# Seven products of a block's first matrix joined in PSUM accumulators instead of on VectorE, in a cross-attention block

## The chip, the core and the metric

The kernel runs on one core of one Trainium2 chip. The time is the device time of the program in microseconds (us); less is better. The runs before the change have a median of 803.14 us (801.75 to 804.53). A core has TensorE (PE, matrix products into the PSUM buffers), VectorE (DVE), ScalarE (ACT), GpSimd (POOL) and SyncE (SP), which here issues most of the DMAs. Each engine works through its own queue in order; semaphores tie them together.

## The reference

A cross-attention block for 4 batches of 512 rows, width 512, 16 heads of 32, inner width 2048, all in float32:

```
x = layer_norm(hidden, ln1_w, ln1_b)
q, k, v = x @ q_w + q_b, enc @ k_w + k_b, enc @ v_w + v_b      # 16 heads of 32
attn = softmax(where(mask, q k^T / sqrt(32), min))
hidden = (attn v) @ cproj_w + cproj_b + hidden
y = layer_norm(hidden, ln2_w, ln2_b)
y = gelu(y @ fc_w + fc_b, approximate=True)                    # 512 -> 2048
out = hidden + y @ proj_w + proj_b                             # 2048 -> 512
```

The change touches `gelu(y @ fc_w + fc_b)`.

## The kernel before

**Attention.** The work is cut into 16 windows, w = 4 * batch + head group (four heads each), and each window into four units of 128 rows, qt; unit u = 4 w + qt runs from 0 to 63. A unit (`scores`, L255, and `turn`, L274) does four score products on TensorE into one PSUM tile of four banks, which has one buffer (pool ps_sc). For each head VectorE adds the mask and takes the row minimum in one reduction (L266), and ScalarE takes the exponential (L270). VectorE transposes two heads at a time (L285, L293); after an odd unit it takes reciprocals (L290), which ScalarE spreads (L292, "rr"). DMAs on SP (L328) exchange blocks of 32 rows, and `attend` (L331, TensorE "av") multiplies by v some units later.

**Filler.** TensorE's other work is put between the units by hand: lists `first[w]` and `later[w]` hold steps with a cost. Where `first[w]` is a tuple it has one list for each unit, run after that unit's scores and turn. Steps are the k, q and v projections (L213 to L234), cproj (L382), the transposes of the second layer norm (L420), and pieces of the feed-forward part: `mlp`, a list of fc and proj steps of batch 0 and of half of batch 1 (SPLIT = 1, FIRST = 2), taken by `some(n)` (a pair counts as two). In windows 13 to 15 these are the only filler. One step of fc makes a tile of 128 of the 2048 columns (`fc`, L532: four products, 512 rows wide, then Gelu on ScalarE); one step of proj makes 128 rows.

**A pair by seven products.** Batch 0's fc, and all fc after attention, take two column tiles at once (`fc_seven`, L483) by Strassen's scheme in Winograd's form: the 512 x 256 block of weights and the 512 x 512 block of y are cut in 2 x 2, and seven half-size products take the place of eight. The sums of weights s1 to s4 are made by `a_sums` (on GpSimd in attention, called by `fc_sums`, L520; on VectorE after it, `sum_wa`, L580), the sums of y, t1 to t4, by `y_sums` (L472), once for a batch. The seven results go to four PSUM tiles, ScalarE copies the first to SBUF (L498), and VectorE joins them by four adds into g (L455); ScalarE's Gelu follows in place (L513). A product is four matmuls in the profile, a pair 28, all with L495 (in `product`).

PSUM: `ps_acc` has four banks for all filler and av; after attention four more, `ps_last`, take the place of the scores.

**Order of weights.** `load_mlp` (L437) loads the tiles of fc and proj in the order of use into a ring of eight, each when the product that last read its place is done; `fc_sums` keeps the weight sums up to two pairs ahead, as soon as the raw weights are asked for.

**After attention** (`last_mlps`, L590): the other half of batch 1's fc and all of batches 2 and 3, pair by pair, each batch followed by its projection, also by seven products (`project`, L613). `load_wa` loads raw weights two pairs ahead.

Of the kernel before, what the change touches and what calls it, by code (L numbers as in the profile page):

```python
# [52 lines left out]
def xattn_block(ctx: ExitStack, tc: tile.TileContext, x, encT, mask, q_w, k_w, v_w, c_w, fc_w, p_w, vecs, rows, out):  # L53
# [201 lines left out]
    def scores(w, qt):  # L255
# [7 lines left out]
        for h in range(HG):  # L263
# [7 lines left out]
            if h % 2:  # L271
                S["ps", w, qt, h // 2] = score_pair()

# [123 lines left out]
    def load_hid(b, ts_):  # L397

        for t in ts_:
            if ("hid", b, t) not in S:  # L400
                S["hid", b, t] = hids.tile([P, D], F32, tag="hid", name=f"hid_{b}_{t}")
            Q[0].dma_start(out=S["hid", b, t], in_=S["xa", b][ts(t, P), :])
        for t in ts_:
# [68 lines left out]
    def y_sums(b):  # L472
        y11, y12, y21, y22 = y_blocks(b)
        e = nc.vector if b else nc.gpsimd
        sub(ys[:, 0], y12, y11)
        sub(ys[:, 1], y22, ys[:, 0])
        sub(y12, y22, y12, e)
        sub(ys[:, 2], y21, ys[:, 1], e)
# [4 lines left out]
    def fc_seven(b, c, g, a, s, half):  # L483
# [4 lines left out]
        q1, q26 = (acc_half(f"{n}_{b}_{c}") for n in ("q1", "q26"))  # L488
        q57, q34 = (half(f"{n}_{b}_{c}") for n in ("q57", "q34"))
        p1 = small.tile([P, HL], F32, tag="p1", bufs=1, name=f"p1_{b}_{c}")  # L490
        g = g.rearrange("p i (j l) -> p (i j) l", j=2)

        def product(o, x, y):
            for k in range(2):
                nc.tensor.matmul(o, x[:, k], y[:, k], start=(k == 0), stop=(k == 1))  # L495

        product(q1[:, 0], a[0][:, 0:2], y11)
        nc.scalar.copy(p1, q1[:, 0])  # L498
        product(q26[:, 0], a[0][:, 2:4], y21)
        product(q26[:, 1], s2, t2)  # L500
        add(nc.vector, g[:, 0:4:3], q26, p1[:, None, :].broadcast_to([P, 2, HL]))
        product(q57[:, 1], s3, t3)
        product(q57[:, 0], s1, t1)
        u2 = g[:, 3:4]
        add(nc.vector, g[:, 1:3], q57, u2.broadcast_to([P, 2, HL]))
        add(nc.vector, g[:, 3], q57[:, 0], g[:, 2])
        product(q34[:, 0], s4, y22)
        product(q34[:, 1], a[1][:, 2:4], t4)
        add(nc.vector, g[:, 1:3], q34, g[:, 1:3])
        for i in range(2):  # L510
            f = 2 * c + i
            h = g[:, 2 * i : 2 * i + 2]
            nc.scalar.activation(h, h, AF.Gelu_apprx_tanh, bias=vec[:, FCB + f : FCB + f + 1], scale=1.0)  # L513

    fc_pairs = [(b, c) for b in range(SPLIT) for c in range(NP)]
# [461 lines left out]
```

## Time and profile before

The profile is of one execution, which took 801.93 us.

| | |
|---|---|
| median of the runs | 803.14 us |
| the profiled execution | 801.93 us, its span 800.2 us |
| mean granted TensorE clock | 0.998 |
| VectorE, line L455 joining a pair in attention (8 pairs) | 3 adds of 512 columns (0.658, 0.692, 0.692 us), 1 of 256 (0.424) |
| VectorE, the same after attention (20 pairs) | 0.684, 0.692, 0.692 and 0.425 us |
| ScalarE, copy of 256 columns out of PSUM (L498) | 0.355 us each, 28 |
| ScalarE, copy of 512 columns out of PSUM (L245) | 0.577 us each, 16 |
| ScalarE, Gelu of 512 columns (L513, L537) | 0.714 and 0.686 us |
| ScalarE, table loads | 1.283 us each, 30 |
| GpSimd, one sum of weights (256 columns) | 0.735 to 0.750 us |
| TensorE, matmul to matmul, 512 and 256 columns | 0.429 and 0.215 us |

In the profile a line is a group of instructions: line, engine, operation, what it writes and reads, shape, count, then busy time and the mean of one in ns, and the idle time just before them with what ended it. Mean durations overlap by some tenths of a microsecond within an engine (matmuls, and the steps of VectorE and ScalarE, are pipelined), so that start to start counts where instructions follow one another. A timeline line begins with start and length in us.

### The profile page before, as it was taken

What the parts mean: (1) busy time and instruction counts of PE and PEld (TensorE: products, weight loads), DVE (VectorE), ACT (ScalarE), POOL (GpSimd) and SP (SyncE); (2) the same over time, 40 slices, a digit from 0 to 9 for tenths busy, and PEclk for the clock granted to TensorE, in tenths of its full rate; (3) what the DMA queues carried; (4) which work ended last, traced back from release to release, by engine and by line L of the source; (5) the groups of instructions that cost most, each with busy time, mean ns of one, the idle gap of its engine ahead of it and who ended that gap; (6) DMA issues with size and microseconds to landing.
All of it is one profiled execution on the core that took longest, in us unless ns stands there. A gap on an engine that the chain in (4) does not pass through costs nothing.

```text
span 800.2 us, 12085 instructions
## 1 busy us (share of the span) xinstructions
PE 785.3 (98%) x4178; PEld 499.4 (62%) x4178; DVE 573.8 (72%) x1179; ACT 339.5 (42%) x745; POOL 123.9 (15%) x146
## 2 busy tenths in 40 slices
PE   9999999989999999999999999999999999999998
PEld 6545455456655645556553433446888888888887
DVE  3789998888888857779878988546738983368511
ACT  2567765547763636456554479500201220022100
POOL 1210030055121141001220100020040020200011
PEclk9999999999999999999999999999999999999999
DMA  8889999847897777787777799882325330033001
GB/s 325 289 230 241 235 237 244 231 115 182 209 240 196 211 210 192 179 198 199 181 173 213 205 261 246 202 254 93 117 84 172 118 106 14 27 86 86 1 14 40
DMA packets 60957, 137.15 MB, mean 171 GB/s; under 512 B 12464, under 2 KB 15664, under 8 KB 60768
## 3 DMA queue, kind: packets, MB, share of 16 engines
q1 hardware_dynamic: 59472, 132.43, 61.3%
q0 software_dynamic: 896, 2.82, 1.1%
q10 hardware_dynamic: 528, 1.14, 0.7%
q8 instruction: 33, 0.54, 0.3%
q14 instruction: 28, 0.23, 0.1%
HBM read 58.22 MB, written 6.82 MB: 81 GB/s over the span
## 4 chain that ended last, share of the span: by engine, by line
PE 87%; DVE 6%; SPq 3%; ACT 1%; issue 1%; DMA 1%; POOL 0%; DVEq 0%; POOLq 0%; ACTq 0%
PE q L495 20%; PE accp L554 8%; PE sc L262 7%; PE accc L386 7%; PE av L345 7%; PE accv L240 6%; PE acck L218 6%; PE accq L228 5%; PE accf L536 3%; DVE ptt L266 3%; SPq L328 2%; PE q4p L622 2%; PE q3p L622 2%; PE q5p L622 2%; PE q6p L622 2%; PE q7p L622 2%
## 5 line engine op out<-in xcount | busy, mean ns | idle before, releaser
L270 ACT ACTIVATE ptt<-ptt,mn 128x512 f32<-128x512 f32 x256 | 181.7, 711 | 135.1 <-DVE mn L266 134.8
L266 DVE CUSTOM_DVE_ANT_0 ptt<-sc,mb 128x512 f32<-128x512 f32 x256 | 161.0, 685 | 32.7 <-PE sc L262 32.4
L285 DVE STREAM_TRANSPOSE tb<-ptt 128x1024 f32<-128x1024 f32 x96 | 119.2, 1242 | 14.4 <-ACT ptt L270 12.9
L554 PE MATMUL accp<-pbt,gt 128*128 128x512 f32 x192 | 86.7, 600 | 0.0
L495 PE MATMUL q<-yT,gt 128*128 128x256 f32 x320 | 78.9, 379 | 0.0
L262 PE MATMUL sc<-pbt 32*128 32x512 f32 x512 | 73.0, 640 | 4.7 <-DVE mn L266 2.5
L513 ACT ACTIVATE ga<-ga,vec 128x512 f32<-128x512 f32 x40 | 26.7, 714 | 93.2 <-DVE ga L455 93.2
L495 PEld LDWEIGHTS q<-yT,gt 128*128 128x128 f32 x320 | 60.8, 190 | 8.7 <-issue 0.5
L554 PEld LDWEIGHTS accp<-pbt,gt 128*128 128x128 f32 x192 | 35.2, 190 | 49.0 <-issue 46.4
L240 PEld LDWEIGHTS accv<-ptt,xe 128*128 128x128 f32 x512 | 58.7, 192 | 9.5 <-issue 6.7
L495 PE MATMUL q<-ys,gt 128*128 128x256 f32 x240 | 61.8, 380 | 0.5 <-DVE ys L452 0.5
L240 PE MATMUL accv<-ptt,xe 128*128 128x128 f32 x512 | 60.8, 277 | 0.0
L218 PE MATMUL acck<-xe,ptt 128*128 128x512 f32 x128 | 59.1, 605 | 0.0
L228 PE MATMUL accq<-xe,ptt 128*128 128x512 f32 x128 | 58.4, 599 | 0.0
L386 PE MATMUL accc<-wc,oT 128*128 128x512 f32 x128 | 56.6, 596 | 0.0
L495 PEld LDWEIGHTS q<-ys,gt 128*128 128x128 f32 x240 | 45.4, 190 | 7.4 <-DVE ys L452 0.9
L345 PE MATMUL av<-pT,v 128*32 128x256 f32 x768 | 48.1, 392 | 1.8 <-DMA gt<-tb 0.7
L498 ACT COPY p<-q 128x256 f32<-128x256 f32 x28 | 9.9, 355 | 92.5 <-PE q L495 92.5
L270 ACT ACTIVATION_READ_ACCUMULATOR ptt<-ptt,mn 128x1 f32 x256 | 47.8, 187 | 0.0
L252 POOL TENSOR_TENSOR v<-v,row 128x512 f32<-128x512 f32 x16 | 20.4, 1275 | 172.9 <-ACT v L245 172.8
L228 PEld LDWEIGHTS accq<-xe,ptt 128*128 128x128 f32 x128 | 23.6, 190 | 32.4 <-issue 30.4
L262 PEld LDWEIGHTS sc<-pbt 32*128 32x128 f32 x512 | 20.0, 182 | 37.9 <-issue 21.4
(137 smaller groups left out, 1071.4 us busy)
## 6 DMA issues: line engine op xcount, KB each, us to landing
pT<-tb SPq DMA_DIRECT2D x384, 136.0 KB, 2.4
pbt<-p_w_dram SPq DMA_DIRECT2D x40, 256.0 KB, 3.1
gt<-fc_w_dram SPq DMA_DIRECT2D x40, 256.0 KB, 2.6
gt<-tb SPq DMA_DIRECT2D x64, 136.0 KB, 3.4
xe<-tb SPq DMA_DIRECT2D x56, 136.0 KB, 3.1
pbt<-fc_w_dram SPq DMA_DIRECT2D x24, 256.0 KB, 3.9
ptt<-k_w_dram SPq DMA_DIRECT2D x16, 256.0 KB, 3.8
xe<-encT_dram SPq DMA_DIRECT2D x16, 256.0 KB, 4.6
```

What stands on the lines that cost most here:

```text
L218: nc.tensor.matmul(acc, S["wk", w][:, d, :], eT[:, d, :], start=(d == 0), stop=(d == ND - 1))
L228: nc.tensor.matmul(acc, S["wq", w][:, d, :], xT[:, d, :], start=(d == 0), stop=(d == ND - 1))
L240: nc.tensor.matmul(acc[:, ts(t, P)], eT[:, d, ts(t, P)], S["wv", w][:, d, :], start=(d == 0), stop=(d == ND - 1),)
L262: nc.tensor.matmul(sc[:, h, :], qT[r, ts(qt, P)], kT[r, :], start=True, stop=True)
L266: nc.vector.tensor_tensor_reduce(out=s, in0=sc[:, h, :], in1=S["mb", w // NG], scale=1.0, scalar=FMAX, op0=ALU.add, op1=ALU.min, accum_out=mn,
L270: nc.scalar.activation(s, s, AF.Exp, bias=mn, scale=-1.0, accum_out=sums[:, qt, h : h + 1])
L285: nc.vector.transpose(*two_heads[k])
L345: nc.tensor.matmul(av[ts(h, HD), : 2 * P].rearrange(shape, **kw), v[:, t, ts(h, HD)], p[t][h], start=(t == 0), stop=(t == NT - 1),)
L386: nc.tensor.matmul(acc, S["oT", b][:, g, ts(t, P)], wc[:, g, :], start=(g == 0), stop=(g == NG - 1))
L495: nc.tensor.matmul(o, x[:, k], y[:, k], start=(k == 0), stop=(k == 1))
L554: nc.tensor.matmul(acc, gT[q % 2][:, k, ts(t, P)], S["pw", b, q * FQ + k], start=(k == 0), stop=(k == FQ - 1))
L622: nc.tensor.matmul(o[:, t], a[:, c, ts(t, P)], w[:, c], start=(c == pairs[0]), stop=(c == pairs[-1]))
```

## The change

Seven parts:

1. `fc_seven` joins the products in three PSUM tiles. qb takes s1 t1 and s3 t3; ScalarE copies both to g[2:4] (512 columns); then s4 y22 and (raw) t4 are added onto qb by TensorE. qa takes a11 y11; ScalarE copies that to g[0]; then a12 y21 is added onto qa. qc takes s2 t2. VectorE makes two adds (256 and 512 columns), GpSimd two (256 columns each). Gelu is three instructions (256, 256 and 512 columns), one of them straight out of PSUM.
2. It is a generator with one stop. `fc_start` runs it up to the stop: four products, the copy of qb, one add. `fc` runs the rest.
3. `scores` takes `middle`: after the second exponential the first step of the unit's list is started, if it is a pair.
4. Half of batch 1's fc (eight tiles in units 57 to 63) goes by pairs too, so that four steps take the place of eight. In windows 14 and 15 the lists become: unit 56 one step, 57 a pair, 58 a pair, 59 none, 60 a pair, 61 none, 62 a pair, 63 two steps. In unit 60 the pair stands behind a load in its list, so it isn't started early.
5. Batch 1's `y_sums` moves from after attention (VectorE) to unit 52 (GpSimd).
6. `fc_sums` issues weight sums when their pair is at most two products ahead of what is done, instead of when the weights are asked for.
7. The adds of proj's bias to rows of batch 1 on GpSimd (`hid_rows`) come one unit after their loads.

```diff
-    def scores(w, qt):
+    def scores(w, qt, middle=None):
...
             if h % 2:
                 S["ps", w, qt, h // 2] = score_pair()
+            if h == 1 and middle:
+                middle()
...
     def y_sums(b):
         y11, y12, y21, y22 = y_blocks(b)
-        e = nc.vector if b else nc.gpsimd
-        sub(ys[:, 0], y12, y11)
-        sub(ys[:, 1], y22, ys[:, 0])
-        sub(y12, y22, y12, e)
-        sub(ys[:, 2], y21, ys[:, 1], e)
+        e, o = ((nc.vector, nc.gpsimd), (nc.gpsimd,) * 2)[b] if b <= SPLIT else (nc.vector,) * 2
+        sub(ys[:, 0], y12, y11, e)
+        sub(ys[:, 1], y22, ys[:, 0], e)
+        sub(y12, y22, y12, o)
+        sub(ys[:, 2], y21, ys[:, 1], o)
...
-        q1, q26 = (acc_half(f"{n}_{b}_{c}") for n in ("q1", "q26"))
-        q57, q34 = (half(f"{n}_{b}_{c}") for n in ("q57", "q34"))
-        p1 = small.tile([P, HL], F32, tag="p1", bufs=1, name=f"p1_{b}_{c}")
+        qb, qa, qc = half(f"qb_{b}_{c}"), acc_half(f"qa_{b}_{c}"), acc_half(f"qc_{b}_{c}")
         g = g.rearrange("p i (j l) -> p (i j) l", j=2)
-
-        def product(o, x, y):
+        u2 = g[:, 0]
+
+        def product(o, x, y, clear=False):
             for k in range(2):
-                nc.tensor.matmul(o, x[:, k], y[:, k], start=(k == 0), stop=(k == 1))
-
-        product(q1[:, 0], a[0][:, 0:2], y11)
-        nc.scalar.copy(p1, q1[:, 0])
-        product(q26[:, 0], a[0][:, 2:4], y21)
-        product(q26[:, 1], s2, t2)
-        add(nc.vector, g[:, 0:4:3], q26, p1[:, None, :].broadcast_to([P, 2, HL]))
-        product(q57[:, 1], s3, t3)
-        product(q57[:, 0], s1, t1)
-        u2 = g[:, 3:4]
-        add(nc.vector, g[:, 1:3], q57, u2.broadcast_to([P, 2, HL]))
-        add(nc.vector, g[:, 3], q57[:, 0], g[:, 2])
-        product(q34[:, 0], s4, y22)
-        product(q34[:, 1], a[1][:, 2:4], t4)
-        add(nc.vector, g[:, 1:3], q34, g[:, 1:3])
-        for i in range(2):
+                nc.tensor.matmul(o, x[:, k], y[:, k], start=clear and k == 0, stop=k == 1, skip_group_check=not clear)
+
+        product(qb[:, 0], s1, t1, True)
+        product(qb[:, 1], s3, t3)
+        nc.scalar.copy(g[:, 2:], qb)
+        product(qa[:, 0], a[0][:, 0:2], y11, True)
+        product(qc[:, 0], s2, t2, True)
+        add(nc.gpsimd, g[:, 3], g[:, 2], g[:, 3])
+        yield
+        nc.scalar.copy(u2, qa[:, 0])
+        add(nc.vector, u2, qc[:, 0], u2)
+        add(nc.gpsimd, g[:, 3], g[:, 3], u2)
+        product(qb[:, 0], s4, y22)
+        product(qb[:, 1], a[1][:, 2:4], t4)
+        add(nc.vector, g[:, 1:3], qb, u2[:, None, :].broadcast_to([P, 2, HL]))
+        product(qa[:, 0], a[0][:, 2:4], y21)
+        for i, o, x in ((0, g[:, 1], g[:, 1]), (0, g[:, 0], qa[:, 0]), (1, g[:, 2:], g[:, 2:])):
             f = 2 * c + i
-            h = g[:, 2 * i : 2 * i + 2]
-            nc.scalar.activation(h, h, AF.Gelu_apprx_tanh, bias=vec[:, FCB + f : FCB + f + 1], scale=1.0)
-
-    fc_pairs = [(b, c) for b in range(SPLIT) for c in range(NP)]
+            nc.scalar.activation(o, x, AF.Gelu_apprx_tanh, bias=vec[:, FCB + f : FCB + f + 1], scale=1.0)
+
+    fc_pairs = [(b, c) for b in range(SPLIT + 1) for c in range(NP if b < SPLIT else FIRST * FQ // 2)]
...
-            if ("fcw", b, 2 * c + 1) not in S:
+            if products.index(("fc", b, *divmod(2 * c, FQ))) > count[1] + 2:
                 return
...
-    def fc(b, f):
...
-    def fc_by_pair(b, c):
+    started = {}
+
+    def fc_start(b, c):
+        if (b, c) in started:
+            return
         q, k = divmod(2 * c, FQ)
-        fc_seven(b, c, gT[q % 2][:, k : k + 2, :], raw_pair(b, c), S["ws", b, c], acc_half)
+        started[b, c] = fc_seven(b, c, gT[q % 2][:, k : k + 2, :], raw_pair(b, c), S["ws", b, c], acc_half)
+        next(started[b, c])
+
+    def fc(b, c):
+        fc_start(b, c)
+        list(started[b, c])
         count[1] += 2
...
-        y_sums(SPLIT)
-
         half = FIRST * FQ // 2
...
     def FC(b, q):
-        if b < SPLIT:
-            return [(2 * CHAIN * 7 / 8, lambda c=c: fc_by_pair(b, c)) for c in range(q * FQ // 2, (q + 1) * FQ // 2)]
-        return [(CHAIN, lambda f=f: fc(b, f)) for f in range(q * FQ, (q + 1) * FQ)]
+        return [(2 * CHAIN * 7 / 8, lambda c=c: fc(b, c), lambda c=c: fc_start(b, c)) for c in range(q * FQ // 2, (q + 1) * FQ // 2)]
...
-    first[13] = some(1), some(1) + stat(2, 0, 1), some(1) + stat(2, 2, 3) + rs(2), some(2)
-    first[14] = some(1) + norm(2, 0, 1), some(1) + norm(2, 2, 3), some(2), some(1)
-    first[15] = hid_(1, 2, 3) + some(1), some(1), some(1), some(2)
+    first[13] = do(lambda: y_sums(1)) + some(1), some(1) + stat(2, 0, 1), some(1) + stat(2, 2, 3) + rs(2), some(2)
+    first[14] = some(1) + norm(2, 0, 1), some(2) + norm(2, 2, 3), some(2), []
+    first[15] = hid_(1, 2, 3) + some(2), do(lambda: hid_rows(1, (2, 3))), some(2), some(2)
...
-            scores(w, qt)
+            now = work[qt] if by_unit else work
+            scores(w, qt, now[0][2] if now and len(now[0]) == 3 and (by_unit or qt < 2) else None)
```

More of the change, by code (lines that the diff above doesn't have):

```diff
@@ L395, in load_xn, with load_hid @@
             Q[0].dma_start(out=S["h", b, t], in_=S["xa", b][ts(t, P), :])
-    def load_hid(b, ts_):
+    def load_hid(b, ts_, rows=True):
         for t in ts_:
@@ L402, in load_hid, with hid_rows @@
             Q[0].dma_start(out=S["hid", b, t], in_=S["xa", b][ts(t, P), :])
+        if rows:
+            hid_rows(b, ts_)
+    def hid_rows(b, ts_):
         for t in ts_:
@@ L530, in fc_sums @@
             count[3] += 1
-    def fc(b, f):
-        q, k = divmod(f, FQ)
-        acc = acc_tile(f"accf_{b}_{f}")
-        for d in range(ND):
-            nc.tensor.matmul(acc, S["fcw", b, f][:, d, :], S["yT", b][:, d, :], start=(d == 0), stop=(d == ND - 1))
-        nc.scalar.activation(
-            gT[q % 2][:, k, :], acc, AF.Gelu_apprx_tanh, bias=vec[:, FCB + f : FCB + f + 1], scale=1.0
-        )
-        count[1] += 1
-        load_mlp()
-    def fc_by_pair(b, c):
-        q, k = divmod(2 * c, FQ)
-        fc_seven(b, c, gT[q % 2][:, k : k + 2, :], raw_pair(b, c), S["ws", b, c], acc_half)
+    started = {}
+    def fc_start(b, c):
+        if (b, c) in started:
+            return
+        q, k = divmod(2 * c, FQ)
+        started[b, c] = fc_seven(b, c, gT[q % 2][:, k : k + 2, :], raw_pair(b, c), S["ws", b, c], acc_half)
[3 more added lines that the diff above has]
+        list(started[b, c])
         count[1] += 2
@@ L609, in fc_pair @@
             sums()
-            fc_seven(b, c, ga[:, c], [wa[c % 2][:, i] for i in range(2)],
-                     [ws[c % 2][:, i] for i in range(4)], half_tile)
+            list(fc_seven(b, c, ga[:, c], [wa[c % 2][:, i] for i in range(2)],
+                     [ws[c % 2][:, i] for i in range(4)], half_tile))
         def project(b, pairs, sums, turns, middle):
@@ L756, in run @@
         while work and (budget is None or spent + work[0][0] / 2 <= budget):
-            cost, fn = work.pop(0)
+            cost, fn, *_ = work.pop(0)
             fn()
@@ L825, in hid_ @@
     def hid_(b, *ts_):
-        return do(lambda: load_hid(b, ts_))
+        return do(lambda: load_hid(b, ts_, False))
     def h_(b, *ts_):
@@ L888, in xattn_block @@
         by_unit = isinstance(work, tuple)
-        share = 0 if by_unit else sum(c for c, _ in work + rest) / NT
+        share = 0 if by_unit else sum(c[0] for c in work + rest) / NT
         due = 0.0
```

## The prediction

> **What bounds the kernel now.** First the page: shares of the engines, then the slices.
>
> ```profile
> span 800.2 us, 12085 instructions
> ...
> PE 785.3 (98%) x4178; PEld 499.4 (62%) x4178; DVE 573.8 (72%) x1179; ACT 339.5 (42%) x745; POOL 123.9 (15%) x146
> ...
> PE   9999999989999999999999999999999999999998
> ...
> DVE  3789998888888857779878988546738983368511
> ...
> PEclk9999999999999999999999999999999999999999
> ```
>
> TensorE is full in nearly every slice; VectorE is near full only in some, ScalarE and GpSimd nowhere. So a saving on VectorE is worth nothing by itself, and a wait put in front of TensorE costs its whole length, because TensorE has no slack later in which to catch up. Second, the chain in order of time gives the prices of TensorE's pieces (start, length).
>
> ```profile
> 173.35 3.61 PE av L345 x32
> ...
> 203.42 6.24 PE q L495 x28
> ...
> 468.29 7.06 PE accf L536 x16
> ...
> 478.29 3.63 PE accf L536 x8
> ```
>
> A pair by seven products is 6.24 us (28 matmuls, one each 0.215); two tiles in full are 7.06 to 7.26. Third, the timeline of the place where batch 1's first tiles run, unit 57 (start, length).
>
> ```profile
> 461.48 1.14 PE L262 MATMUL sc<-pbt 32*128 32x512 f32 x8
> ...
> 462.55 3.70 PE L536 MATMUL accf<-yT,pbt 128*128 128x512 f32 x8
> ...
> 464.57 0.68 DVE L266 CUSTOM_DVE_ANT_0 ptt<-sc,mb 128x512 f32<-128x512 f32 x1
> ...
> 465.30 0.72 ACT L270 ACTIVATE ptt<-ptt,mn 128x512 f32<-128x512 f32 x1 [3.74 <-DVE mn L266]
> ...
> 467.01 0.08 DVE L266 DVE_READ_ACCUMULATOR2_ANT mn<- 128x1 f32 x1
> ...
> 467.15 1.14 PE L262 MATMUL sc<-pbt 32*128 32x512 f32 x8 [0.90 <-DVE mn L266]
> ...
> 468.26 0.20 DVE L290 RECIPROCAL rsum<-sums 128x8 f32<-128x8 f32 x1
> 468.38 1.19 DVE L293 STREAM_TRANSPOSE tb<-ptt 128x1024 f32<-128x1024 f32 x1
> 468.50 0.40 ACT L292 COPY rr<-rsum 128x256 f32<-128x256 f32 x1 [0.27 <-DVE rsum L290]
> ```
>
> Three things are to be seen. The scores tile has one buffer: the next unit's scores (467.15) start only when the fourth reduction's accumulator is read (467.09), 2.5 us after the first reduction starts. What TensorE does meanwhile is the 3.6 us of other work placed between. And VectorE is already late here: scores end at 462.55, reductions start at 464.57. Exponentials start 0.73 after the first reduction and run 0.71 apart.
>
> **The change in units 57 to 63** (batch 1's fc). Removed: eight tiles, in the chain 6 x 3.63 + 7.06 = 28.8 us. Added: four pairs, 4 x 6.24 = 25.0. TensorE's work falls by **3.9**, and the 0.90 stall above goes, since 6.24 stands between those two scores. But eight pieces become four. They go to units 57, 58, 60 and 62, so units 59 and 61 have none: their scores are followed at once by the next scores, which must wait for four reductions. And each pair now has two waits of TensorE on ScalarE inside it: its fifth product accumulates onto the buffer that ScalarE's 512-wide copy reads (0.58, as L245's copy of that size), its seventh onto the one that the 256-wide copy reads (0.36, L498). The first copy stands in ScalarE's queue behind two exponentials (four in unit 60, where the work list begins with a load and so the early start doesn't apply); the second stands behind the other exponentials, and in odd units behind the rr copy, which waits for VectorE's reciprocal. By the row of 203.42 TensorE wants the fifth product 3.56 after the scores' end and the seventh 1.73 later. Going through it with these rows, in the times of the trace:
>
> - Unit 57: exponentials from 465.30, second ends 466.72, copy to 467.4; TensorE wants 466.1: waits 1.3. Exponentials end 468.8, reciprocal, rr copy 469.5, second copy 469.9 against 469.1: 0.8. Pair ends 470.85.
> - Unit 58: scores end 471.9. VectorE's transposes, two adds and two norms (0.98) put the reductions at 472.4; ScalarE has a table load, Gelus until 472.9, a table load (1.28) until 474.2, two exponentials, copy until 476.2; wanted at 475.45: 1.05 with the second copy. Pair ends 479, av (1.87), scores of 59 end 482.0.
> - Unit 60's scores wait for reductions 482.1 to 484.6: 2.7.
> - Unit 60: VectorE's transposes of unit 59 (2.8) hold its reductions to 487.5, the four exponentials end 491.1, copy 491.7, wanted 489.3: 2.4. Pair ends 494.3, scores of 61 497.2.
> - Unit 62's scores wait for reductions until 499.9: 2.6.
> - Unit 62: reductions 502.6 after transposes, copy 505.35, wanted 504.45: 1.1 with the second copy.
>
> Stalls: 2.1 + 1.05 + 2.7 + 2.4 + 2.6 + 1.1 = 12.0. Net **12.0 - 0.9 - 3.9 = +7.2**. After this TensorE runs projections without a wait, as before.
>
> **Batch 0's eight pairs** (units 22 to 45). The count of matmuls is the same. VectorE loses two 512-wide and one 256-wide add and gains one 256-wide (four adds, 2.5 us, become 1.1), ScalarE gains a 512-wide copy and splits a Gelu in two (512-wide: 0.71). A 256-wide Gelu out of PSUM has no row: 0.36 (copy of that size) to 0.71; 0.4 taken, the size decides. GpSimd gains two 256-wide adds (0.73 each): with batch 1's and the tail's 32 pairs, 47 us on an engine busy 124 of 800. They delay only the last Gelu; without that cover a Gelu would hold the next unit's exponentials by 0.7. Accumulating into a used bank is bounded by today's second matmuls of a product, which accumulate at the same 0.215: nothing. VectorE's relief hits no stall of TensorE, so it is worth nothing here. The same two copy waits apply: unit 23, straight after another pair, 0.65 + 0.9, so that av begins at 192.85 instead of 192.28, where its present wait of 0.69 for a buffer goes: 0.55; the odd units 25, 33, 37, 45 wait 0.2, 0.3, 0.35, 0.45 for the second copy behind rr. Sum **+1.9** (0 if ScalarE is earlier, 4 if every pair loses 0.5).
>
> **GpSimd's moved steps.** y_sums(1) goes from VectorE to GpSimd in unit 52, four ops of 1.26 to 1.78, 5.8 us, 30 us ahead of its reader; behind it stand the stores of out, whose adds come later anyway. Weight sums issued later (3.0 each): those of pair 0 stand behind the second store (issued 457.7) and end by 461.3, before 462.6. Pairs 2 and 3 sum at 474 and 480, needed at 485.8 and 500.9. The weights' loads keep their place in SP's queue (that of pair 0 issued at 453.02, landed 456.7). Row adds of hid come later, needed after 510. All nothing; a late one would cost its lateness.
>
> **Tail.** There ScalarE and VectorE have gaps, so the copies hide (copy done 2.4 into a pair, wanted at 3.5).
>
> ```profile
> PE tp L159 <- ACT pbt L231: 3.0, 1, 3.0
> PE sc L262 <- DVE mn L266: 2.5, 2, 1.6
> ...
> PE q L495 <- DVE ys L452: 0.5, 1, 0.5
> ```
>
> The last line's 0.5 goes (batch 1's sums are ready). The first projection matmul waits 0.4 at 575.8 for the last Gelu; the last add now lies before the last product, so that goes. But the first product is now s1 t1 instead of raw weights: at 601.2, batch 2's start, VectorE ends the first weight sum at 602.33, so TensorE loses 1.15. Batch 3's start has 2 us to spare. Sum **+0.25**.
>
> **Sum**: 7.2 + 1.9 + 0.25 = +9.3. On the profiled execution (801.93, span 800.2, 1.7 around it) that is 811.3; it stands 1.2 under the median of the runs, 803.14, so the forecast is **811**.
>
> **Half clock.** The waits above show one TensorE gap of 3.0; the windows show what followed (the number before the last two is the granted clock).
>
> ```profile
> 80.00:100.00 20.00, 18.35 (x124) 9.57 (x120) 18.64 (x44) 14.32 (x37) 1.27 (x1) 1.00 0.93 235
> 160.00:180.00 20.00, 16.94 (x114) 10.58 (x113) 16.51 (x36) 8.82 (x19) 11.57 (x13) 0.91 0.45 114
> ```
>
> After the gap of 3.0 the clock fell (0.91), and the av at 173.35 took 3.61 instead of 1.87, 1.7 more; the gap of 1.6 at 82 left 1.00. My gaps of 2.4 to 2.7 lie between. [...] The 3.0 row already paid, so each of three gaps may cost 0 to 1.7; I take 0 and keep 5 for the range.
>
> **Rivals.**
> (1) *The saved work wins.* If scores are released head by head, or ScalarE runs well ahead, the six stalls shrink; the kernel gains from the point where they sum to under about 5. With none, -3.9 - 0.9 - 0.9 = -5.7: 796. Against it: 467.09 to 467.15 shows the release after the fourth reduction. Chance 0.10.
> (2) *Only the two empty boundaries cost*, 2.5 each, the copies being hidden: 5.0 + 1.15 - 5.7 = +0.45: 802.4. It needs VectorE on time; the row at 464.57 has it 2 us late. Chance 0.12.
> (3) *The gaps trip the half clock*: 811 + 1.7 to 5.1, 813 to 816, with longer waits to 819. Chance 0.13.
> (4) *Forecast*, 805.5 to 815: chance 0.65.
>
> Range 803 to 818: leaves out (1), part of (2) and the end of (3). Less than 0.3% (2.4 us) can't be told from no change: faster 0.10, same 0.12, slower 0.78.
>
> **What would show it.** Right: TensorE waits of 2 to 3 us before scores of units 60 and 62, by DVE mn; waits of the new matmul line on ACT of 0.3 to 2.4 inside pairs; the fifth of the span with batch 1's fc longer by some 7; TensorE back to back from there but for 1 us at batch 2's start; VectorE's sum down by some 35. Wrong: no wait before those scores, or TensorE stalled on POOL or a DMA instead, which would mean that the moved sums are late.

## The result, and the profile after

The changed kernel takes **816.38 us** (median; 815.33 to 817.45) against 803.28 before in the same series: a ratio of **1.0164**, 95% interval 1.0142 to 1.0186, 13.1 us slower. The forecast was 811, with a range of 803 to 818: the sign and the mechanism were right, and the forecast was 5 short. The profiled execution of the changed kernel is its slowest (817.45, span 815.6), that of before one of its faster ones (801.93); between these two there are 15.5.

The page of the changed kernel, shares of the engines and slices:

```profile
span 815.6 us, 12279 instructions
...
PE 790.4 (97%) x4226; PEld 512.7 (63%) x4226; DVE 540.5 (66%) x1127; ACT 359.6 (44%) x809; POOL 187.6 (23%) x230
...
PE   9999899989999999999999987999999999999998
...
DVE  3788998777678857679868987625436873346411
...
PEclk9999999989999999999999997999999999999999
```

VectorE's sum falls from 573.8 to 540.5, as meant, and it buys nothing. In slices 24 and 25 (about 470 to 510) TensorE falls to 8 and 7, and the granted clock to 7 in the second. The waits of TensorE in the changed kernel (total, times, longest):

```profile
PE sc L262 <- DVE mn L266: 6.9, 3, 2.7
PE qb L500 <- ACT gt L504: 3.4, 3, 2.1
...
PE qb L500 <- DVE gt L461: 1.1, 1, 1.1
...
PE qa L500 <- ACT gt L509: 0.4, 1, 0.4
```

The first line was 2.5 before: the wait of 0.90 is gone, and two waits of 2.7 are new. The second and the last are TensorE's waits on the two copies, the third is batch 2's start. And the timeline of TensorE in units 57 to 63 (start, length, and idle before with its releaser at the end), the stretch that before ran from 461.48 to 504.29 with one stall of 0.90:

```profile
466.89 1.14 PE L262 MATMUL sc<-pbt 32*128 32x512 f32 x8
...
473.80 1.88 PE L500 MATMUL qb<-yT,wsum 128*128 128x256 f32 x4 [2.12 <-ACT gt L504]
475.47 1.91 PE L500 MATMUL qb<-ys,pbt 128*128 128x256 f32 x4
477.18 1.14 PE L500 MATMUL qa<-yT,pbt 128*128 128x256 f32 x4
...
491.55 2.09 PE L262 MATMUL sc<-pbt 32*128 32x512 f32 x8 [2.66 <-DVE mn L266]
493.57 2.08 PE L500 MATMUL qb<-ys,wsum 128*128 128x256 f32 x4
495.44 1.91 PE L500 MATMUL qb<-yT,pbt 128*128 128x256 f32 x4
...
507.58 1.62 PE L262 MATMUL sc<-pbt 32*128 32x512 f32 x8 [2.65 <-DVE mn L266]
509.13 2.08 PE L500 MATMUL qb<-ys,wsum 128*128 128x256 f32 x4
...
519.47 0.70 PE L557 MATMUL accp<-pbt,gt 128*128 128x512 f32 x1
```

Four matmuls of a product take 1.03 to 1.13 at full clock; after each gap they take 1.9 to 2.1 (granted clock 0.50 there, from 473.97, 491.04 and 508.11 on). The stretch is now 52.58 long (466.89 to 519.47) instead of 42.81: **+9.8** of the 15.5. The rest by the starts of the scores: 1.7 at unit 20, where av waits 1.61 for a weight of v that lands late (it stands before anything that changed, and differs between the kernels below, in which it is the same, by 0.0 to 1.7, so it isn't the change's); 0.7 of other small steps before unit 22; 3.05 from unit 22 to unit 50, where batch 0's pairs run; -0.1 from the first accp (+15.2) to the last matmul (+15.1), and 0.3 behind that. Without the 2.4 that stand ahead of unit 22, 9.8 + 3.05 + 0.3 make 13.1, which is what the medians differ by.

### The profile page after: what moved, and what is told of

Its sections match the earlier page's. It is cut to its first block, busy times and chain, and to the rows that moved or that the text cites. A ratio compares the mean times of both kernels' runs of the same rounds, so it can differ in the third digit from the quotient of the medians.

```text
span 815.6 us, 12279 instructions
## 1 busy us (share of the span) xinstructions
PE 790.4 (97%) x4226; PEld 512.7 (63%) x4226; DVE 540.5 (66%) x1127; ACT 359.6 (44%) x809; POOL 187.6 (23%) x230
## 3 DMA queue, kind: packets, MB, share of 16 engines
q10 hardware_dynamic: 528, 1.14, 0.7%
## 4 chain that ended last, share of the span: by engine, by line
PE 76%; SPq 9%; DVE 7%; DMA 3%; ACT 2%; issue 2%; POOL 0%; DVEq 0%; POOLq 0%
PE qb L500 13%; PE accp L557 9%; SPq L330 8%; PE qa L500 6%; PE sc L262 6%; PE av L347 5%; PE accc L388 5%; PE accv L240 5%; PE acck L218 4%; PE accq L228 3%; PE qc L500 3%; DVE ptt L266 3%; PE q5p L625 2%; PE q3p L625 2%; PE q7p L625 2%; PE q6p L625 2%
## 5 line engine op out<-in xcount | busy, mean ns | idle before, releaser
L262 PE MATMUL sc<-pbt 32*128 32x512 f32 x512 | 75.0, 656 | 9.1 <-DVE mn L266 6.9
L461 POOL TENSOR_TENSOR ga<-ga 128x256 f32<-128x256 f32 x40 | 30.2, 756 | 119.8 <-ACT ga L504 82.9
L504 ACT COPY ga<-qb 128x512 f32<-128x512 f32 x20 | 11.7, 585 | 101.1 <-PE qb L500 58.2
L518 ACT ACTIVATE ga<-ga,vec 128x256 f32<-128x256 f32 (+1 forms) x40 | 24.4, 609 | 62.1 <-DVE ga L461 62.1
L388 PEld LDWEIGHTS accc<-wc,oT 128*128 128x128 f32 x128 | 23.7, 190 | 31.5 <-issue 29.1
L218 PEld LDWEIGHTS acck<-xe,ptt 128*128 128x128 f32 x128 | 23.4, 192 | 31.6 <-issue 29.3
L500 PE MATMUL qb<-ys,gt 128*128 128x256 f32 x160 | 41.2, 380 | 1.1 <-DVE gt L461 1.1
```

The lines of the kernel that those rows point to most:

```text
L218: nc.tensor.matmul(acc, S["wk", w][:, d, :], eT[:, d, :], start=(d == 0), stop=(d == ND - 1))
L262: nc.tensor.matmul(sc[:, h, :], qT[r, ts(qt, P)], kT[r, :], start=True, stop=True)
L388: nc.tensor.matmul(acc, S["oT", b][:, g, ts(t, P)], wc[:, g, :], start=(g == 0), stop=(g == NG - 1))
L500: nc.tensor.matmul(o, x[:, k], y[:, k], start=clear and k == 0, stop=k == 1, skip_group_check=not clear)
```

## The experiments

Theory A: the loss sits in units 57 to 63, in the two unit boundaries without filler, the waits on ScalarE's copies in the pairs, and the half clock that the gaps bring. Rivals: batch 0's and the tail's joins; the half clock alone; the copies alone; or engines that are late in these units whatever the order. All ratios are to the kernel before in the same series, with 95% intervals (its median there is 803.3 to 804.5, so ratios are to be compared, not medians); the last column is the stretch from unit 57's scores to the first projection after unit 63 in the trace (before: 42.81), in the runs marked * less 7.26 for the two projection steps of 3.63 that were moved into it.

| run | what | median | ratio | stretch |
|---|---|---|---|---|
| changed kernel | | 816.38 | 1.0164 (1.0142 to 1.0186) | 52.58 |
| e1 | batch 1's tiles in full again | 807.96 | 1.0046 (1.0020 to 1.0071) | 42.80 |
| e6 | before, but batch 1 by pairs, old join | 811.63 | 1.0094 (1.0071 to 1.0118) | 50.35 |
| e2 | pairs in halves | 819.38 | 1.0178 (1.0158 to 1.0199) | 54.19 |
| e3 | 20 dummy matmuls in each gap | 815.47 | 1.0144 (1.0123 to 1.0165) | 52.41 |
| e8 | 9 dummy matmuls in each gap | 815.95 | 1.0143 (1.0119 to 1.0166) | 50.94 |
| e9 | first copy after one exponential | 817.26 | 1.0167 (1.0148 to 1.0186) | 51.62 |
| e10 | raw products first in the tail | 815.46 | 1.0156 (1.0135 to 1.0176) | 52.60 |
| e7 | projections in the gaps | 816.66 | 1.0160 (1.0143 to 1.0178) | 47.08* |
| f1 | pairs first, projections between | 814.53 | 1.0150 (1.0130 to 1.0169) | 43.29* |
| f2 | f1, norms later | 814.18 | 1.0136 (1.0113 to 1.0159) | 41.30* |
| f3 | f2, old join in batch 0, raw first in the tail | 812.61 | 1.0118 (1.0102 to 1.0133) | 41.31* |
| f5 | f2, old join in batch 0, two weight tiles by GpSimd's queue | 805.68 | 1.0024 (1.0009 to 1.0039) | 41.30* |

### Where: e1 and e6

e1 undoes parts 4 and 5 of the change alone; the main lines:

```diff
-    fc_pairs = [(b, c) for b in range(SPLIT + 1) for c in range(NP if b < SPLIT else FIRST * FQ // 2)]
+    fc_pairs = [(b, c) for b in range(SPLIT) for c in range(NP)]
...
-    first[14] = some(1) + norm(2, 0, 1), some(2) + norm(2, 2, 3), some(2), []
+    first[14] = some(1) + norm(2, 0, 1), some(1) + norm(2, 2, 3), some(2), some(1)
```

> The changed kernel with one part undone: batch 1's eight fc tiles in units 57 to 63 go one by one again, in the units of the kernel before, and batch 1's sums of y go back to VectorE after attention. Batch 0's pairs and the tail keep the new join. Theory A (most of the +13.1 comes from units 57 to 63, by the two unit boundaries without filler, the waits on ScalarE's copies inside the pairs, and the half clock after the gaps; from the profiles +5.41 at unit 57's scores against +15.2 at the projections, so 9.8 there): 816.4 less 9.8 less a possible disturbance, 804 to 807. Rival R1 (the new join itself costs, in batch 0's eight pairs and the twenty of the tail): hardly below the changed kernel, 811 to 816. Rival R2 (nothing outside units 57 to 63 costs anything): 803.

807.96, a little above the range of theory A; by its ratio, 1.0046 of 803.3, it is 807.0, at the end of the range. The stretch is that of before (42.80). Units 22 to 50 lose 2.7 here (0.83 to 3.51 behind before). The rest of this trace, which is of one of the slower executions (809.15), is the experiment's own: with batch 1's sums of y back after attention, the new order wants t1 in the first product; first accp to the first projection matmul of the tail takes 73.36 instead of 70.21, TensorE's waits there led by 1.4 for VectorE's ys, with one window at half clock behind them (granted clock 0.996 over this execution). So e1 places the loss: with the tiles back, the stretch loses nothing, and 2.7 at most are batch 0's.

e6 does parts 4 to 7 without 1 to 3: batch 1's pairs in the same units, joined in the old way and never started early.

> The kernel before with batch 1's eight tiles made as four pairs in units 57, 58, 60 and 62 as in the changed kernel, but joined in the old way, by four adds on VectorE; the sums of y and of weights and the rows of the bias stand where the changed kernel has them. Theory A: the two empty boundaries cost 2.65 each, the half clock after them up to 1.7 each, now not covered by waits on copies, VectorE's longer joins something; less 3.9 of products and the old 0.9 stall: 803.3 + 5.3 + 3.4 - 4.8 = 807, range 803 to 811. Rival R6 (the two copies on ScalarE inside a pair make nearly all of the loss): 803.3 + 5.3 - 4.8 or less, 798 to 804. Rival R7 (the placement makes all of it, whatever the join): 811 to 814.

811.63, above theory A's 807. By its ratio, 1.0094 (1.0071 to 1.0118) of 803.3, it is 810.8 (809 to 812.8), where theory A's range ends and R7's begins, so the median does not choose between them. R6 falls: the copies of the new join are not nearly all of it. The placement with the old join makes 7.5 of the stretch's 9.8, so not quite all, as R7 would have it, but more than theory A gave it. TensorE's waits in e6:

```profile
PE sc L262 <- DVE mn L266: 7.9, 3, 3.4
PE av L345 <- ACT p L502: 4.1, 3, 2.5
```

The boundaries wait longer than in the changed kernel (3.42 and 2.85), because VectorE's four adds stand ahead of the reductions. The second line was not expected: with the old join the wait on ScalarE only moves, from the fifth product to the av behind the pair (2.47 and 0.94), whose PSUM bank is free only when ScalarE's late copy has read the first product.

### The half clock: e3 and e8

Both put matmuls of the identity, whose result nobody reads, into the two gaps (20 and 9 of them):

```diff
+    def idle():
+        spare = acc_tile("spare")
+        for _ in range(9):
+            nc.tensor.matmul(spare[:, :P], ident, ident, start=True, stop=True)
...
-    first[14] = some(1) + norm(2, 0, 1), some(2) + norm(2, 2, 3), some(2), []
+    first[14] = some(1) + norm(2, 0, 1), some(2) + norm(2, 2, 3), some(2), do(idle)
```

> The changed kernel with 20 matmuls of the identity (128 columns each, about 2.1 us in all, result unused) put into the two boundaries without filler, after units 59 and 61, where TensorE only waits. The waits stay as long as they are, only the clock can change. Theory A: both gaps shrink to about half a microsecond, the clock stays full there, and of the 5.1 us of TensorE time lost at half speed after them only the part that isn't covered by the copy waits comes back, 0.9 for each pair: 816.4 - 1.8 = 814.6. Rival R4 (the half clock is the main loss): 816.4 - 5 = 811 or less. Rival R5 (the gaps do not cause the half clock, or all of it lies under other waits): 816.4.

> As the run with 20 dummy matmuls, but with 9 in each of the two boundaries: those 20 took 4.73 us instead of 2.1 (0.236 each) and made each boundary 2.0 longer, which paid back what the clock gained (units 57 to 63: 52.41 against 52.58). Nine take 2.1, less than the wait of 2.65, so only the clock changes. Theory A (the half clock of units 60 and 62 is partly covered by the waits on the copies): 816.4 - 1.8 = 814.6. Rival R4 (it costs its whole length, 2.12 and 1.64 by unit lengths against the run with 20): 816.4 - 3.8 = 812.6. Rival R5 (no effect of the clock): 816.4.

The 20 took 4.73 instead of 2.1, so that each boundary became 1.9 longer; still the stretch did not (52.41 against 52.58), with the clock at 1.00 in it (0.87 in the changed kernel): the 3.9 us of useless work were paid by the half clock, which was gone, and by shorter waits on the copies of units 60 and 62 (0.69 and none; in e8, below, 2.13 and 0.71). As a measure of the clock alone this run failed, by its size, and its median (815.47) tells nothing apart. With 9, TensorE in e8:

```profile
469.40 1.10 PE L500 MATMUL qb<-yT,wsum 128*128 128x256 f32 x4 [2.14 <-ACT gt L504]
...
478.45 1.10 PE L500 MATMUL qb<-yT,wsum 128*128 128x256 f32 x4 [0.92 <-ACT gt L504]
...
484.14 2.27 PE L745 MATMUL spare<-ident 128*128 128x128 f32 x18
486.87 1.14 PE L262 MATMUL sc<-pbt 32*128 32x512 f32 x8 [0.45 <-DVE mn L266]
...
493.79 1.10 PE L500 MATMUL qb<-yT,wsum 128*128 128x256 f32 x4 [2.13 <-ACT gt L504]
...
499.48 2.27 PE L745 MATMUL spare<-ident 128*128 128x128 f32 x18
502.20 1.14 PE L262 MATMUL sc<-pbt 32*128 32x512 f32 x8 [0.45 <-DVE mn L266]
...
507.71 1.10 PE L500 MATMUL qb<-yT,wsum 128*128 128x256 f32 x4 [0.71 <-ACT gt L504]
```

The granted clock of this execution was 1.000: here all the waits can be read at full clock. The waits on the copies in units 60 and 62, which the changed kernel's trace does not show, were there all the time under the half clock (2.13 and 0.71). The stretch is 50.94, so by these two traces the half clock adds **1.6** to it in the changed kernel, as theory A expected (1.8), not R4's 3.8. This one execution took 811.41. The median does not show it, because other executions of the same kernel had the half clock: by granted clock, 811.41 at 1.000; 813.66 at 0.998; 815.48 and 816.52 at 0.996; 816.42 and 817.32 at 0.994. One window of 3.41 at half clock (0.50 in the changed kernel's trace) is at most 1.7 us, or 0.2% of the span; three of them would be the 5 us between the first and the last. In which stretch these windows lie is not known, as only one execution has a trace. So with 9 dummies the half clock is rarer by the mean clock (0.994 to 1.000, against 0.987 to 0.996 in the changed kernel), not impossible, and the median of e8 leaves the choice between its theories open; the one trace makes it.

The 811.41 is not the changed kernel less its new half clock alone. Before the scores of unit 22, after the wait of 3.05 that all these kernels have there, the kernel before ran one window at half clock in its trace and the changed kernel two; e8 ran none, and is 1.6 ahead of before at that point. From there on it loses 2.6 to unit 50, 8.1 in the stretch and 0.3 behind it: 11.0, less the 1.6, is its 9.4 over the span of before.

### Filling the gaps with halves: e2

```diff
+            return [(CHAIN, lambda c=c, step=step: step(b, c)) for c in range(q * FQ // 2, (q + 1) * FQ // 2) for step in (first_half, fc)]
```

> The changed kernel with the four pairs of batch 1 cut in two: the first four products and both copies in one unit, the last three products in the next, in units 57/58, 59/60, 61/62 and 63, so that every unit boundary has filler again. No work is taken away. Theory A: the two empty boundaries (2.66 and 2.65), the copy waits (2.1 in unit 57, and by the ends of the copies about 0.5, 2.3 and 0.8 more that the half clock covered) and what the half clock added (about 3.2) go, 14 in all: 816.4 - 14 = 802.5, range 800 to 806, and the granted clock stays full between 466 and 520. Rival R1 (the join elsewhere costs): 811 or more. Rival R3 (ScalarE and VectorE are too late in these units whatever the order): the waits come back in the same sum at other places, 810 to 816.

A miss by 17: the slowest of all, 819.38. TensorE's waits and, from ScalarE's timeline of unit 60, what stood ahead of the copy:

```profile
PE qb L500 <- ACT gt L504: 10.4, 6, 3.8
PE sc L262 <- DVE mn L266: 4.3, 3, 1.8
```

```profile
486.23 0.72 ACT L270 ACTIVATE ptt<-ptt,mn 128x512 f32<-128x512 f32 x1
...
488.36 0.71 ACT L270 ACTIVATE ptt<-ptt,mn 128x512 f32<-128x512 f32 x1
...
489.43 0.40 ACT L294 COPY rr<-rsum 128x256 f32<-128x256 f32 x1 [0.27 <-DVE rsum L292]
489.74 0.58 ACT L504 COPY gt<-qb 128x512 f32<-128x512 f32 x1
```

The halves have no early start, so the copy stands behind four exponentials and rr, and ScalarE reaches those a unit late. The boundaries shrank from 5.3 to 2.6, the waits on the first copy grew to 10.4 over the whole trace (7.1 in e8, at full clock). Theory A in its simple form (fill the gaps and the 14 us come back) falls; R3 was right on this order, though its range (810 to 816) was too low. What the gap gives back, the next late engine takes.

### The copies' place: e9

```diff
-            if h == 1 and middle:
+            if h == 0 and middle:
```

> The changed kernel with the early start of a pair after the first exponential instead of the second, so that ScalarE's copy of the first two products stands behind one exponential. Theory A (the fifth product's wait is the copy's place in ScalarE's queue): the copy comes 0.7 earlier; the waits of 0.54 (unit 23) and 0.67 (unit 26) go, 0.7 of the 2.1 in unit 57 goes, some 0.3 in units 58 and 62: -2.2, so 814.2; the sum of waits of the matmul line on that copy falls from 3.4 to about 1.4. Rival R9 (the exponentials behind the copy come 0.6 later and hand the loss on to the transposes, the exchange and the next unit): 816 or more, with new waits of scores or av.

```profile
PE qa L500 <- ACT gt L509: 3.6, 7, 1.1
PE qb L500 <- ACT gt L504: 3.3, 5, 1.4
```

No gain (817.26). The wait in unit 57 fell from 2.1 to 1.4, but the exponentials behind the copy came later, the second copy behind them too, and the seventh products' waits rose from 0.4 (one) to 3.6 (seven); the sum on the first copy stayed (3.3 against 3.4). A place in a full queue is only exchanged.

### The tail: e10

```diff
+        if raw:
+            product(qa[:, 0], a[0][:, 0:2], y11, True)
         product(qb[:, 0], s1, t1, True)
```

> The changed kernel with the products of the raw weights (a11 y11) first in the pairs after attention. Theory A (the first product s1 t1 has to wait for the first weight sum at batch 2's start, 1.06 in the trace): that wait goes, 816.4 - 1.1 = 815.3. Rival R10 (the tail has other waits behind it, as the copy of a11 y11 is wanted again by the seventh product): 816.4.

The median (815.46) is theory A's number, but its interval takes in the changed kernel's, so it decides nothing; the trace does. The wait of 1.06 at batch 2's start shrinks to 0.2, but the tail from the first accc to the end gets longer, 261.5 against 260.6: now only one product, not two, lies between the first copy and the fifth product, whose first matmul lasts 0.46 instead of 0.38, so that the sixth product starts 0.95 after it instead of 0.86, in each pair. Twenty times 0.09 is more than the 0.86 saved. Rival R10 was right, by another copy than it named.

### Filling the gaps with real work: e7, f1, f2, f3, f5

e7 puts two projection steps of batch 1, from behind unit 63, into the gaps (f0 and f1 are batch 1's pairs, p0 the first half of its projection):

```diff
-    mlp += FC(SPLIT, 0) + FC(SPLIT, 1) + PJ(SPLIT, 0) + PJ(SPLIT, 1)
+    mlp += f0 + p0[:1] + f1[:1] + p0[1:2] + f1[1:] + p0[2:] + PJ(SPLIT, 1)
...
-    first[14] = some(1) + norm(2, 0, 1), some(2) + norm(2, 2, 3), some(2), []
+    first[14] = some(1) + norm(2, 0, 1), some(2) + norm(2, 2, 3), some(2), some(1)
```

> The changed kernel with two steps of batch 1's projection (3.6 us of TensorE work each, which in the changed kernel ran after unit 63) moved into the two unit boundaries without filler, after units 59 and 61; the steps after unit 63 are respread by as much. No work is added or taken away. Theory A (these two boundaries, with the half clock that follows them, hold most of the loss): 7.3 leaves the end of attention, each boundary grows from 2.65 to 3.6, so -5.3, and the half clock after units 59 and 61 goes, -1.8 to -3.7: 816.4 - 7.1 to 9.0 = 807 to 809. Rival R8 (the projections were needed as cover at the end of attention): as much comes back there as waits of av, 812 to 816. Rival R3 (ScalarE and VectorE are too late in these units whatever the order, as the pairs in halves suggest): the copy waits in units 60 and 62 grow by what the gaps lose, 811 to 815.

```profile
PE accp L566 <- DMA pbt<-p_w_dram: 7.2, 2, 4.3
PE qb L509 <- ACT gt L513: 5.4, 6, 2.1
```

816.66, no gain. The boundaries' waits went, and two waits for weights came (2.94 in unit 59, 4.25 after unit 63). The first loads were issued at 486.83 to 488.96, straight behind 16 copies of an exchange in SP's queue (475.61 to 486.71); the second, all but one, from 529.90 on, when TensorE had ended the projections before them (529.70), as a ring of eight places would have it. R8's sum, but not its mechanism.

f1 puts the pairs into units 57, 58, 59 and 61 and the projections into 60, 62 and 63; f2 also moves batch 2's norms from units 56 and 57 to 62 and 63; f3 also joins batch 0's pairs in the old way and puts the raw products first in the tail. The lists of f2 and f3:

```diff
-    first[14] = some(1) + norm(2, 0, 1), some(2) + norm(2, 2, 3), some(2), []
-    first[15] = hid_(1, 2, 3) + some(2), do(lambda: hid_rows(1, (2, 3))), some(2), some(2)
+    first[14] = some(1), some(2), some(2), some(2)
+    first[15] = hid_(1, 2, 3) + some(1), some(2) + do(lambda: hid_rows(1, (2, 3))), some(1) + norm(2, 0, 1), some(2) + norm(2, 2, 3)
```

> The changed kernel with batch 1's steps in another order: pairs in units 57, 58, 59 and 61, projection steps in units 60, 62 and 63, so that no boundary is empty, and no projection stands where its weights have not landed (the run with projections in the gaps waited 2.94 and 4.25 for weights, because a place in the ring of eight comes free only when the pair that read it is done). Two projection steps fewer remain after unit 63. No work is added or taken away. Theory A (the empty boundaries and the half clock they bring hold most of the loss): 803.3 + 2.7 for batch 0's joins - 4.8 for the products saved and the old stall + 4 to 5 for waits on copies = 805.6, range 803 to 809. Rival R3 (ScalarE and VectorE are too late in these units whatever the order): three pairs in a row bring waits on copies of 2 and more in each, 811 to 815. Rival R8 (the projections were needed as cover at the end of attention): 811 or more, as waits of av.

> As the run before in this list, and batch 2's four rows of the second norm (0.98 each on VectorE) move from units 56 and 57 to 62 and 63, where no pair follows. In the trace they stand ahead of the reductions of units 57 and 58, whose exponentials and so the first copies come late. Theory A (the copy waits of 2.13 + 0.31 in unit 57 and 0.92 in unit 58 come from VectorE's queue): 805.6 - 3.0 = 802.6, or 3 less than the run before, whatever that is. Rival R11 (the copies' place behind the exponentials is what costs, VectorE being on time or not): no more than 1 less.

> As the run before in this list, with batch 0's eight pairs joined in the old way (four adds on VectorE, no copy of qb) and the raw products first in the pairs after attention. Theory A: 2.7 of batch 0 (unit 22 to 50 in the trace of the run with full tiles) and 1.1 at batch 2's start go: 802.6 - 3.8 = 798.8, which would beat both kernels; 3.8 less than the run before, whatever that is. Rival R12 (what batch 0 shows is the half clock's phase and DMA arrivals, not the join): 1.1 less than the run before.

In the stretch all goes as theory A has it: 43.29 in f1, 41.30 in f2 (the norms were 2.0 of it; unit 57's wait on the first copy of 2.1 is gone), 1.5 less than before. But the medians hardly move (814.53, 814.18, 812.61) and miss theory A's 805.6, 802.6 and 798.8. In f3 units 22 to 57 lose 1.8 less than in f2 (the join of batch 0), and the tail, with the raw products first, 0.5 more. f2's SP queue and TensorE tell why (the SP line of 504.19 merges 16 copies, the last one of which is issued at 524.38):

```profile
500.38 1.02 SPq L456 DMA_DIRECT2D pbt<-p_w_dram  x2
501.51 0.84 SPq L404 DMA_DIRECT2D hid<-xa  x2
504.19 20.69 SPq L330 DMA_DIRECT2D pT<-tb  x16
524.99 3.06 SPq L456 DMA_DIRECT2D pbt<-p_w_dram  x6
```

```profile
512.15 8.85 PE L563 MATMUL accp<-pbt,gt 128*128 128x512 f32 x20
527.97 6.84 PE L563 MATMUL accp<-pbt,gt 128*128 128x512 f32 x12 [6.97 <-DMA pbt<-p_w_dram]
```

TensorE comes to the last projections two steps earlier, and their last two weights stand in SP's queue behind the last window's exchange. The wait is 7.0, the 7.26 that was moved; two windows run at half clock (0.83 from 520 to 540), the first of them while TensorE still waits. f1 and f3 show the same, with waits of 6.0 and 7.2. f5 takes f2 with the old join in batch 0, and loads these two tiles by another queue:

```diff
-            Q[0].dma_start(out=w, in_=fc_w[:, f, :, :] if name == "fc" else p_w[ts(f, P), :])
+            q = nc.gpsimd if (name, b) == ("p", SPLIT) and f in (FQ + 2, FQ + 3) else Q[0]
+            q.dma_start(out=w, in_=fc_w[:, f, :, :] if name == "fc" else p_w[ts(f, P), :])
```

> As the run with the old join in batch 0, but the last two weight tiles of batch 1's projection are loaded by GpSimd's queue instead of SP's, where they stand behind 16 copies of the last exchange and are issued only at 525 (TensorE waits 7.2 for them in that run); the products after attention have the changed kernel's order again (the raw products first gave nothing in the runs with them). Theory A' (what was taken out of the gaps came back as this wait and the half clock of 0.83 that follows it): 812.6 - 7.2 - 1.5 = 804, range 802.5 to 806, and no wait of accp on a DMA; with all waits on copies but 2 gone this would be the whole of the loss, and the saved products (3.9) no more than pay for the waits left. Rival R13 (the exchange of the last window isn't done earlier whatever TensorE has to do; av waits for it in place of the weights): 809 to 812, with waits of av on the exchange of 4 or more.

805.68, ratio 1.0024, inside the range of theory A', and no wait on these weights is left: of the 13.1 all but 2 are gone, and the executions are within 3 us of each other at clocks of 0.997 to 1.000. It does not beat the kernel before. TensorE at the end of attention in f5:

```profile
511.86 1.14 PE L262 MATMUL sc<-pbt 32*128 32x512 f32 x8
512.93 14.00 PE L600 MATMUL accp<-pbt,gt 128*128 128x512 f32 x32
527.96 1.93 PE L347 MATMUL av<-pT,v 128*32 128x256 f32 x32 [1.03 <-DMA pT<-tb]
529.83 7.13 PE L600 MATMUL accp<-pbt,gt 128*128 128x512 f32 x16
538.53 1.93 PE L347 MATMUL av<-xe,v 128*32 128x256 f32 x32 [1.57 <-DMA pbt<-x_dram]
```

Now av itself waits, 1.03 and 1.57: the chain of work runs through the last exchange there (520.2 to 534.7, four weight loads of SP within it), and fewer matmuls ahead of it do not bring it earlier; the second wait the profile puts down to a load of x that stands behind the exchange in SP's queue. From the first projection to the first accc this costs 3.1 against before, the 7.26 moved counted in. The whole of this trace, 4.65 over before in span: 1.5 ahead of unit 22, 1.35 from there to unit 57, -1.5 in the stretch, 3.1 for the exchange, 0.1 behind it.

## Why the prediction was right in sign and short in size

**TensorE is the bound; a wait ahead of it costs its length.** Right. VectorE lost 33 us of work for nothing.

**Work saved in units 57 to 63, -3.9 and -0.9.** Mostly there, once the waits are gone: f2's stretch is 1.5 shorter than before with 1.9 of idle time left in it (0.25 + 0.31, 0.92, 0.11 + 0.31), so 3.4 of the 4.8; from start to start these five waits delay by 2.7, which makes 4.2. But only f1 to f5 show it, and f5 shows that it isn't worth its length: behind it stands the exchange.

**The stalls, 12.0.** Right as a sum, by e8 at full clock and the changed kernel: unit 57 2.14 + 0.31 (forecast 2.1), 58 0.92 (1.05), before 60 2.66 (2.7), 60 2.13 (2.4), before 62 2.65 (2.6), 62 0.71 (1.1), in all 11.5 of idle time; from start to start, 12.5. The split in unit 57 was wrong: nearly all is the first copy, because the two norms of unit 56 (1.97 in the trace) stand ahead of the reductions; f2, which moves them, takes 2.0 off.

**The half clock, "each of three gaps may cost 0 to 1.7; I take 0".** This is the term that was set too low. Three gaps of 2.12, 2.66 and 2.65 were followed by one, two and one windows at half clock. In the profiled executions they add 1.6 to the stretch (52.58 against e8's 50.94). So of the stretch's 9.8 the forecast had 7.2, the half clock made 1.6, and 0.9 are small errors of the two terms above (12.5 - 4.4 = 8.1 in e8). Rival (3) happened in its number, 813 to 816 and with longer waits to 819, and in part of its mechanism; it was given 0.13 where the forecast had 0.65. The 0 was the author's estimate, and no run shows it for these gaps: the changed kernel's trace has windows at 0.50 behind all three. Behind some other gaps of such a length there were none: 2.13 in e3, 2.14 and 2.13 in e8, 2.47 and 2.85 in e6, where only the scores behind 3.42 took 2.09 instead of 1.14.

**The sum.** The +9.3 was added to the profiled execution of before, 801.93, though the result is compared with the median, 803.14: on that the same sum gives 812.4, not 811. So of the 5.4 that the forecast was short, 1.4 are this step (the median of before is 803.28 in the series of the result), 2.6 the stretch, 1.15 the units of batch 0, and the rest rounding, if the stretches of the one trace stand for the medians. That one execution of e8 took 811.41 is no confirmation of 811: it had none of the half clock that before itself has ahead of unit 22.

**Batch 0, +1.9.** About right for the join: 2.7 in e1 and 3.05 in the changed kernel between units 22 and 50, of which some 0.9 to 1.35 come with the old join too (f3, e6, f5), so about 1.7 for the join. In the other traces with the same join in batch 0 the whole is 2.6 to 4.4. But the same steps, 0.67 in unit 23, 0.94 in unit 26, -0.37 in unit 27 and 0.23 in unit 37, 1.5 in all, stand in each of these nine traces and in none of the three with the old join. Unit 26 was not foreseen; the odd units' waits for the second copy came out smaller (0 to 0.23). The Gelu of 256 columns, taken at 0.4, takes 0.46 out of PSUM and 0.51 otherwise. A run with only batch 0's old join beside the changed kernel was not made.

**GpSimd's moved steps, nothing.** Right: no wait of TensorE on GpSimd but the one at the start; in f2, where pairs start sooner, the first such shows, 0.25 for a weight sum.

**Tail, +0.25.** Measured -0.1 to the last matmul, +0.3 to the end of the span; the 1.06 at batch 2's start was foreseen (1.15).

**Rival (1), saved work wins**, falls: it needed stalls of under 5, and they were 11.5; no arrangement with pairs in batch 1 came below the kernel before. **Rival (2), only the empty boundaries**, falls: without them (f1) waits of copies, weights and the exchange stay.

What stays open: e6's 7.5 mixes the placement with VectorE's longer join; how often each execution meets the half clock, and where, is known only from the mean clock of a few executions; and in f5 the remaining 2 are split by one trace alone, of one of its slower executions (806.59).

## What to carry to other kernels

Filler that TensorE does between latency chains is also their cover: before taking matmuls out, ask in each boundary which chain is due and whether the rest still covers it, here 3.6 us of work against 2.65 of reductions. When gaps are refilled, follow the work to where it came from: a ring of weights, a queue in order and the last exchange each took the gain back once. And price a gap of TensorE at its length, and look at the granted clock behind it: here one or two windows of 3.41 at half clock came behind gaps of 2.12, 2.66 and 2.65 in the changed kernel, none behind 2.13 in e3 and 2.85 in e6 (the next section has the busy shares at which it was met).

## What the hardware showed

In the traces of before and of the changed kernel the granted clock is 1.00 or 0.50, and its changes are multiples of 3.41 us apart: half clock runs from 173.44 to 176.86 in before, and from 173.60 to 180.43, 473.97 to 477.39, 491.04 to 497.87 and 508.11 to 511.52 in the changed kernel, and in the idle last 0.3 of its span. Laid out over the span in cells of 3.41, this grid has a cell that begins at 81.28 in before and one at 81.44 in the changed kernel; and in none of the five cells at full clock ahead of half clock was TensorE idle throughout (busy for 0.74 to 1.38). Cells of the changed kernel's grid, each row one window (PE busy is the first number after the length, granted clock the third from the end):

```profile
470.56:473.97 3.41, 1.29 (x7) 0.84 (x6) 3.41 (x11) 2.30 (x6) 2.37 (x4) 1.00 0.88 279
473.97:477.39 3.42, 3.42 (x9) 2.71 (x9) 2.60 (x5) 3.07 (x7) 0.68 (x2) 0.50 0.92 283
...
487.63:491.04 3.41, 1.26 (x12) 0.31 (x8) 2.50 (x8) 3.33 (x7) 2.14 (x3) 1.00 0.75 218
491.04:494.46 3.42, 2.91 (x10) 1.32 (x11) 3.41 (x7) 2.00 (x7) 0.00 (x0) 0.50 0.37 134
494.46:497.87 3.41, 3.41 (x9) 2.69 (x9) 3.41 (x9) 2.94 (x9) 0.00 (x0) 0.50 0.71 153
497.87:501.28 3.41, 3.41 (x17) 2.99 (x17) 1.75 (x4) 2.11 (x3) 1.45 (x2) 1.00 0.96 216
```

A cell in which TensorE was busy for 1.29 or 1.26 of 3.41 is followed by one at 0.50; a cell at half clock that is busy for 2.91 is followed by another, one that is busy throughout by a full one. Over these two executions, counted from TensorE's records: of 460 cells at full clock the five with TensorE busy for 0.22 to 0.41 of the cell were each followed by half clock, and the 455 others, busy for 0.52 and more, by full clock; of the seven at half clock the two busy for 0.70 and 0.85 were followed by another, the five busy throughout by a full one. So in these two traces it is the busy share of the cell that tells what follows (between 0.41 and 0.52 they have no cell), and a gap of 2.1 paid or not by how it fell on the grid: that of unit 57 paid in the changed kernel (a cell busy 0.38) and not in e3, where it was as long (2.13) and its emptiest cell was busy 1.99 of 3.41:

```profile
474.18:477.59 3.41, 1.99 (x9) 1.46 (x9) 2.92 (x7) 3.12 (x10) 0.82 (x2) 1.00 0.89 233
```

The wait ahead of unit 22, 3.05 in before, 3.06 in the changed kernel and 3.1 in e8, had no fixed price either: in before its cell was busy 0.74 of 3.41 and one cell at 0.50 followed, in the changed kernel 1.38 and two followed, and in e8, with a granted clock of 1.000 over the execution, none.

With useless matmuls in the gaps the clock stayed up in both executions: with 4.73 us of them in each boundary e3's stretch had a clock of 1.00 (0.87 in the changed kernel) and was no longer than the changed kernel's (52.41 against 52.58), though 1.5 longer than e8's, whose 2.27 us fill no more than the wait.
